# Four graph layers on one core: two of three batch norms folded early, the last batch's bias and norm by halves

## The chip, the cores and the metric

The kernel runs on one NeuronCore of a Trainium2 chip. The metric is the device time of one execution in microseconds. The core has five engines with their own in-order queues: PE (TensorE: matmuls and transposes, writing to PSUM), DVE (VectorE), ACT (ScalarE), POOL (GpSimd) and SP (which here only issues DMAs). In the profile, PEld is PE's weight load, listed apart.

## The reference, cut to what matters

Sixteen graphs ("batches") of 1024 nodes with 128 features go through four layers; each layer's result is added to its input and normalised over the features.

```python
x = layernorm(x + L0(x, adj))           # attention over neighbours, gated
x = layernorm(x + L1(x, adj, nodemask)) # dilated adjacency, three SAGE steps with batch norm
x = layernorm(x + L2(x, adj))           # attention over neighbours, gated
x = layernorm(x + L3(x, adj))           # two-step graph convolution with elu
```

The change concerns layer 1's output and the very end of layer 3:

```python
h1 = bn(relu(sage(x,  adj_d, ...)), g1, be1)   # bn: mean and variance over all batches and nodes
h2 = bn(relu(sage(h1, adj_d, ...)), g2, be2)
h3 = bn(relu(sage(h2, adj_d, ...)), g3, be3)
y  = concat([h1, h2, h3], -1) @ Wl + bl        # then layernorm(x + y)
...
out = norm_A @ (h @ W2) + b2                   # layer 3, then layernorm(x + out)
```

A batch norm is, once its statistics are known, a scale and a shift of each feature: h = a * n + s. So the product with Wl is n @ (a * Wl) plus a constant s @ Wl, which belongs to the bias.

## The kernel before

Each batch is held as 8 blocks of 128 rows, either by rows ("xn", "yn", "n": 128 partitions x 8 x 128) or transposed ("hT", "yT", "xT": 128 x 1024). Most work on a batch goes by two halves of 512 columns, one PSUM bank each. The helpers `turned` (L753: transposes through PE), `products` (L761: matmuls with a 128x128 weight) and `halves` (L747) yield one such half after another; `spans(fine)` (L803) yields two halves or the whole. `normed` (L786) is the layer norm: statistics and aggregates on DVE, the power -1/2 on POOL, then one ACT activation for each block of 128 rows.

Each layer is written as a few streams for each batch (Python generators) which `take_turns` and `in_turn` (L810, L814) interleave. The order written there is not yet the order on an engine: a scheduler in the tile framework arranges the instructions of each engine, and waits for buffers follow from pools of a fixed number of tiles.

Layer 1's third step (`Step`, loop over the 16 batches in the order 8 to 15, 0 to 7) has for each batch: load hT and ag on SP's queue (L1348, L1350); `out` (L1388 and after) with 32 matmuls of 128x128 (L1397), bias on DVE ("o", L1399), squares on ACT (L1405), row sums ("ss", L1406), "rn" (L743, power on POOL at L744, L1409) and "n" (L1413); `keep` (L1417 and after) with transposes (L758), copies "nT" (L1422), batch norm statistics (L1423) and a store of nT to DRAM (h2T_d, L1424, on POOL's queue). After all batches `norm` (L1325) turns the statistics into bn_ab[2], whose column 0 is the scale and column 1 the shift (L1327 to L1332). bn_ab[0] and bn_ab[1] have been known since the first and second step.

`Layers23` holds what layers 2 and 3 need. Its weights are loaded during layer 1's third step (`weights`, L1200), and `load` (L1229) brings a batch: adjacency A8, the three un-normed outputs hb0, hb1, hb2 (one buffer each, so a batch's hb can be loaded only when the products of the batch before have read it), and xn. `take_norms` (L1220) folds the three norms into bias and Wl: three matmuls into "pc" (L1224), an addition to blcol (L1225), three scalings of Wl (L1227).

Layer 2's `before` for a batch is: products of Wl with hb (L1547), yT with the bias (L1548), transposes, yn and xn (L1551, L1554), layer norm, then xT, hT, G and hn for the attention. Two batches run `before` at the start of layer 2, with attention behind. `attention` uses the PSUM pool ps_w for "pmm" and ps_a for "acc"; everything else goes through ps_h (tag "h", two banks). In layer 1, ps_h has four banks and ps_a four.

At the end of layer 3 (`after`), `propagated` gives "prop" by halves (L1536, L1538), one ACT instruction adds the bias c2 (L1667), then prop is transposed and added to xn (L1670), normed, and stored (L1673; for the last batch by halves, on SP's queue).

Of the kernel before, what the change touches and what calls it, by code (L numbers as in the profile page):

```python
# [9 lines left out]
F32 = mybir.dt.float32  # L10
# [6 lines left out]
AF = mybir.ActivationFunctionType  # L17
OP = mybir.AluOpType
AX = mybir.AxisListType
PSUM = bass.MemoryType.PSUM  # L20
DRAM = bass.MemoryType.DRAM

P = 128
# [616 lines left out]
def fast_kernel(ctx: ExitStack, tc: tile.TileContext, t: dict, out: bass.AP, flag: bass.AP):  # L640

    nc = tc.nc
    B, N, D = t["x"].shape
    NT = N // P
    H2 = N // 512
# [40 lines left out]
    def nat(ap):  # L686
        return ap.rearrange("(t p) d -> p t d", p=P)
# [7 lines left out]
    def column(pool, src, name):  # L695
        v = pool.tile([P, 1], F32, name=name)
        nc.sync.dma_start(v, bass.AP(tensor=src.tensor, offset=src.offset, ap=[[1, P], [1, 1]]))
        return v
# [62 lines left out]
    def products(psum, *pairs):  # L761

        for p, c, _ in halves(psum):
            for i, (W, x) in enumerate(pairs):
                nc.tensor.matmul(p, W, x[:, c], start=(i == 0), stop=(i == len(pairs) - 1))  # L765
            yield p, c
# [16 lines left out]

        return v[:, :, None].to_broadcast([P, 4, P])

    def normed(small, r, fine=False):  # L786

        for k in spans(fine):
            n = k.stop - k.start
            st = small.tile([P, NT, 6], F32, name="ln_st")  # L790
            mv = small.tile([P, NT, 2], F32, name="ln_mv")
            for i in range(n):
                nc.vector.bn_stats(st[:, i, :], r[:, k.start + i, :])  # L793
            for i in range(n):
                nc.vector.bn_aggr(mv[:, i, :], st[:, i, :])
            rstd = power_mhalf(small, mv[:, :n, 1], add=LN_EPS, name="ln_rstd")
            nb = small.tile([P, NT], F32, name="ln_nb")
            nc.vector.scalar_tensor_tensor(nb[:, :n], mv[:, :n, 0], -1.0, rstd, op0=OP.mult, op1=OP.mult)  # L798
            for i in range(n):
                nc.scalar.activation(r[:, k.start + i, :], r[:, k.start + i, :], AF.Identity,  # L800
                                     scale=rstd[:, i:i + 1], bias=nb[:, i:i + 1])

    def spans(fine):  # L803

        return [slice(0, NT // 2), slice(NT // 2, NT)] if fine else [slice(0, NT)]
# [384 lines left out]
    class Layers23:  # L1190
# [8 lines left out]
        def weights(self, ps_h):  # L1199
            wts = self.wts  # L1200
            self.Wl = wts.tile([P, 3, P], F32, name="Wl")
            nc.sync.dma_start(self.Wl, nat(t["L1_gnn_Wl"]))
            self.blcol = column(wts, t["L1_gnn_bl"], "blcol")
            self.W2T = transposed(wts, ps_h, matrix(wts, t["L2_gnn_W_w"], "l2W"), "l2WT", "h")
            self.b2 = column(wts, t["L2_gnn_W_b"], "l2b")
            self.As2 = symmetric(wts, ps_h, matrix(wts, t["L2_gnn_A"], "l2A"), "l2As", "h")
            self.gw = wts.tile([P, 2, 32], F32, name="l2gw")
            nc.vector.memset(self.gw, 0.0)
            self.gb = wts.tile([P, 3], F32, name="l2gb")
            for i, n in enumerate(("ig", "fg", "og")):  # L1210
                with nc.allow_non_contiguous_dma(reason="a vector of 256"):
                    nc.sync.dma_start(self.gw[:, :, i], t[f"L2_gnn_{n}_w"].rearrange("o (h d) -> d (o h)", d=P))
                src = t[f"L2_gnn_{n}_b"]
                nc.sync.dma_start(self.gb[:, i:i + 1], bass.AP(tensor=src.tensor, offset=src.offset, ap=[[0, P], [1, 1]]))
            self.U = [matrix(wts, t[f"L3_gnn_W{i}"], f"U{i}") for i in range(3)]
            self.c = [column(wts, t[f"L3_gnn_b{i}"], f"c{i}") for i in range(3)]
            self.nbig = wts.tile([P, 1], F32, name="nbig")
            nc.vector.memset(self.nbig, -BIG)

        def take_norms(self, psum):  # L1220

            pc = psum.tile([P, 1], F32, name="pc", tag="h")
            for l in range(3):
                nc.tensor.matmul(pc, self.Wl[:, l, :], bn_ab[l][:, 1:2], start=(l == 0), stop=(l == 2))  # L1224
            nc.vector.tensor_add(self.blcol, self.blcol, pc)  # L1225
            for l in range(3):
                nc.vector.tensor_scalar(self.Wl[:, l, :], self.Wl[:, l, :], bn_ab[l][:, 0:1], None, op0=OP.mult)  # L1227

        def load(self, s, b):  # L1229
            s.A8 = self.ins.tile([P, NT, N], FP8, name="A8", bufs=3)  # L1230
# [255 lines left out]
    with ExitStack() as ph:  # L1486
        work = ph.enter_context(tc.tile_pool(name="l2_work", bufs=1, reuse_waits="tile"))
        small = ph.enter_context(tc.tile_pool(name="l2_small", bufs=3, reuse_waits="tile"))
        ps_w = ph.enter_context(tc.tile_pool(name="l2_pw", bufs=2, space=PSUM, reuse_waits="tile"))
        ps_a = ph.enter_context(tc.tile_pool(name="l2_pa", bufs=1, space=PSUM, reuse_waits="tile"))  # L1490
        ps_h = ph.enter_context(tc.tile_pool(name="l2_ph", bufs=2, space=PSUM, reuse_waits="tile"))

        W2T, b2, As2, gw, gb, nbig, blcol, Wl = l2.W2T, l2.b2, l2.As2, l2.gw, l2.gb, l2.nbig, l2.blcol, l2.Wl
        (U0, U1, U2), (c0, c1, c2) = l2.U, l2.c
# [46 lines left out]
        def before(s, b):  # L1541

            if b:
                l2.load(s, b)
            yield
            yT = wide("yT")
            for p, c in products(ps_h, *((Wl[:, l, :], s.hb[l]) for l in range(3))):  # L1547
                nc.scalar.activation(yT[:, c], p, AF.Identity, bias=blcol)  # L1548
            yn = rows("yn", 2)
            for p, c, k in turned(ps_h, yT):  # L1550
                nc.vector.tensor_mul(yn[:, k, :], tiles3(p), half_rows(mf[:, b * NT + k.start:b * NT + k.stop]))  # L1551

            for k in spans(b < 2):
                nc.vector.tensor_add(s.xn[:, k, :], s.xn[:, k, :], yn[:, k, :])  # L1554
            yield
            normed(small, s.xn, b < 2)
            yield
            s.xT = wide("xT", 2)
            for p, c, _ in turned(ps_h, s.xn):
                nc.scalar.copy(s.xT[:, c], p)  # L1560
            yield
            s.hT = wide("hT", 2)
            for p, c in products(ps_h, (W2T, s.xT)):
                nc.scalar.activation(s.hT[:, c], p, AF.Identity, bias=b2)
            yield
            s.G = wide("G", 2)
            for p, c in products(ps_h, (As2, s.hT)):
                nc.scalar.copy(s.G[:, c], p)
            s.hn = wide("hn", 2)
            for p, c, _ in turned(ps_h, s.hT):  # L1570
                nc.vector.tensor_copy(s.hn[:, c], p)
            yield
# [31 lines left out]
        def after(s, b):  # L1604
# [14 lines left out]
            last = b == B - 1  # L1619
# [44 lines left out]
            parts = scaled_parts(h2, U2, db)  # L1664
            yield
            r = propagated(parts, A, dB)
            nc.scalar.activation(r, r, AF.Identity, bias=c2)  # L1667
            yield
            for p, c, k in turned(ps_h, r):
                nc.vector.tensor_add(s.xn[:, k, :], s.xn[:, k, :], tiles3(p))  # L1670
            normed(small, s.xn, last)
            for k in spans(last):
                (nc.sync if last else nc.gpsimd).dma_start(nat(out[b])[:, k, :], s.xn[:, k, :])  # L1673
            yield
# [49 lines left out]
```

## Time and profile before

| | |
|---|---|
| median of 4 runs | 3015.39 us (3008.26 to 3020.5) |
| profiled execution | 3010.69 us |
| its span, first to last instruction | 3009.0 us |
| mean granted TensorE clock | 0.972 |
| busy: PE, DVE, ACT, POOL | 91%, 77%, 67%, 11% |
| chain that ended last: PE, DVE, issue, ACT, DMA, POOL | 37%, 22%, 21%, 9%, 6%, 5% |

All durations are from the one profiled execution; its time is the span and 1.7 us around it. A busy share is a mean over stages that have different limits, so what a place costs is read in that place: in the timeline (start, duration, engine, line, output<-inputs, and in brackets how long the engine had been idle and for whom it waited) and in the chain of waits, which goes back from the last instruction to whatever released each step. A PE row with "x2" for one product of 128x512 is one matmul: the f32 product is recorded as two.

### The profile page before, as it was taken

To read this page: it belongs to the slowest core of one execution; us is meant where nothing else is said; L and a number is where in the kernel's file an instruction comes from. 1 tells how busy PE (TensorE), PEld (TensorE's weight loads), DVE (VectorE), ACT (ScalarE), POOL (GpSimd) and SP (SyncE) were. 2 spreads that over 40 slices of the span, in tenths; PEclk is the share of its full clock that TensorE was granted. 3 is DMA by queue.
4 is the path that set the end of the run, shared out by engine and by line. 5 is a ranking of instruction groups with operands and counts; after the bars stand their busy time and mean duration, and the time that the engine had idled before them with its cause. 6 is when DMAs were issued, how large, how long until landed. Compare 5 with 4: busy or idle time off the path is not lost.

```text
span 3009.0 us, 42998 instructions
## 1 busy us (share of the span) xinstructions
PE 2737.2 (91%) x15219; PEld 1719.9 (57%) x15282; DVE 2329.7 (77%) x5987; ACT 2028.2 (67%) x3475; POOL 326.0 (11%) x295
## 2 busy tenths in 40 slices
PE   7999999996999998998999987999999999999995
PEld 3444444443566666887788874455555555555554
DVE  6898898887999995776688885766777777777765
ACT  5777787784788777666555535766666676676763
POOL 0000000003000001121122231000010001000000
PEclk9999999998999999999999998999999999999998
DMA  5344444431000014223367692111111111111000
GB/s 163 126 161 148 133 147 154 147 128 42 2 2 2 2 76 164 90 99 128 128 238 243 229 350 88 36 56 57 63 70 60 64 69 68 56 57 57 22 15 23
DMA packets 124128, 297.96 MB, mean 99 GB/s; under 512 B 12672, under 2 KB 65664, under 8 KB 116736
## 3 DMA queue, kind: packets, MB, share of 16 engines
q1 hardware_dynamic: 103440, 211.65, 21.1%
q0 software_dynamic: 20464, 83.47, 7.4%
q8 instruction: 122, 2.00, 0.3%
q14 instruction: 102, 0.84, 0.1%
HBM read 211.04 MB, written 84.02 MB: 98 GB/s over the span
## 4 chain that ended last, share of the span: by engine, by line
PE 37%; DVE 22%; issue 21%; ACT 9%; DMA 6%; POOL 5%; SPq 0%; POOLq 0%; DVEq 0%; ACTq 0%
PE ph L1536 8%; PE acc L1293 7%; PE ph L765 5%; PE acc L1601 4%; DMA an<-in_adj 4%; PE ph L1397 3%; PE pmm L723 3%; POOL ln_rstd L744 3%; ACT xn L800 3%; DVE ln_st L793 3%; PE ph L758 3%; PE ph L1522 2%; DVE em L1587 2%; ACT em L969 2%; PE acc L976 2%
## 5 line engine op out<-in xcount | busy, mean ns | idle before, releaser
L723 PE MATMUL pmm<-G,hT 128*128 128x512 f32 x1024 | 506.0, 611 | 7.7 <-DVE mx L1587 5.0
L800 ACT ACTIVATE xn<-xn,ln_nb,ln_rstd 128x128 f32<-128x128 f32 x512 | 207.6, 481 | 115.5 <-DVE ln_nb L798 115.5
L723 PEld LDWEIGHTS pmm<-G,hT 128*128 128x128 f32 x1024 | 179.1, 193 | 175.9 <-issue 140.5
L976 PE MATMUL acc<-em,hs 128*128 128x512 f32 x512 | 244.8, 602 | 16.4 <-DVE hs L973 14.3
L1293 PE MATMUL acc<-a,lo 128*128 128x512 f32 x768 | 243.4, 401 | 16.0 <-DVE lo L1260 16.0
L744 POOL TENSOR_TENSOR ln_rstd<-ln_rstd,mhalf 128x8 f32<-128x8 f32 (+1 forms) x68 | 113.5, 1670 | 1327.5 <-DVE ln_rstd L741 607.6
L1601 PE MATMUL acc<-em,hs 128*128 128x512 f32 x512 | 250.4, 608 | 3.6 <-DVE hs L1598 1.9
L1293 PE MATMUL acc<-a,hi 128*128 128x512 f32 x768 | 244.0, 402 | 3.7 <-ACT hi L1259 3.5
L1140 ACT ACTIVATE q<-s,negc 128x512 f16<-128x512 f32 x256 | 170.4, 696 | 59.6 <-DVE negc L1119 22.3
L922 ACT ACTIVATE ab<-an 128x1024 bf16<-128x1024 f32 x128 | 134.6, 1052 | 109.6 <-DMA an<-in_adj 71.0
L1138 PE MATMUL s<-step,carry 128*128 128x384 bf16 (+3 forms) x1034 | 199.4, 304 | 7.9 <-DVE carry L1108 3.2
L1152 ACT ACTIVATE carry<-pc,negone 128x512 fp8e4<-128x512 f32 x256 | 166.6, 698 | 38.5 <-PE pc L1151 29.1
L965 DVE CUSTOM_DVE_ANT_0 em<-pmm,msk 128x1024 f32<-128x1024 f32 x128 | 156.1, 1219 | 31.5 <-PE acc L976 26.3
L1293 PEld LDWEIGHTS acc<-a,lo 128*128 128x128 f32 x768 | 144.1, 190 | 55.2 <-DVE lo L1260 21.6
L1587 DVE CUSTOM_DVE_ANT_0 em<-pmm,msk 128x1024 f32<-128x1024 f32 x128 | 155.8, 1217 | 25.7 <-PE acc L1601 21.2
L925 DVE SCALAR_TENSOR_TENSOR chk<-an 128x1024 fp8e4<-128x1024 f32 x128 | 156.4, 1222 | 17.4 <-DMA an<-in_adj 17.1
L1293 PEld LDWEIGHTS acc<-a,hi 128*128 128x128 f32 x768 | 143.0, 190 | 37.1 <-ACT hi L1259 4.0
L1582 ACT ACTIVATE msk<-A,nbig 128x1024 bf16<-128x1024 fp8e4 x128 | 145.8, 1140 | 26.7 <-DVE mx L1587 23.4
L930 DVE TENSOR_SCALAR carry<-pt 128x1024 fp8e4<-128x1024 bf16 x128 | 155.7, 1217 | 6.8 <-PE pt L929 6.8
L1397 PE MATMUL ph<-Wx,hT 128*128 128x128 f32 x768 | 152.1, 281 | 5.0 <-DVE l2WT L709 3.2
L976 PEld LDWEIGHTS acc<-em,hs 128*128 128x128 f32 x512 | 91.2, 191 | 113.2 <-issue 87.8
L969 ACT ACTIVATE em<-em,nmx 128x1024 f32<-128x1024 f32 x128 | 146.8, 1147 | 12.3 <-DVE nmx L967 11.8
(289 smaller groups left out, 6256.6 us busy)
## 6 DMA issues: line engine op xcount, KB each, us to landing
an<-in_adj SPq DMA_DIRECT2D x128, 512.0 KB, 4.2
adj_d<-carry POOLq DMA_DIRECT2D x16, 1024.0 KB, 5.0
A<-dil_d SPq DMA_DIRECT2D x16, 1024.0 KB, 6.7
rdeg<-rdeg_d SPq DMA_DIRECT2D x32, 512.0 KB, 4.3
ag_d<-ag POOLq DMA_DIRECT2D x32, 512.0 KB, 5.3
ag<-ag_d SPq DMA_DIRECT2D x32, 512.0 KB, 6.0
A<-adj_d SPq DMA_DIRECT2D x16, 1024.0 KB, 4.7
xn<-in_x SPq DMA_DIRECT2D x16, 512.0 KB, 4.2
```

Source lines behind the costliest of these rows:

```text
L723: nc.tensor.matmul(p[:, h * 512:(h + 1) * 512], lhsT, rhs[:, h * 512:(h + 1) * 512], start=True, stop=True)
L744: nc.gpsimd.tensor_tensor(r, r, mhalf[:, :n], op=OP.pow)
L800: nc.scalar.activation(r[:, k.start + i, :], r[:, k.start + i, :], AF.Identity, scale=rstd[:, i:i + 1], bias=nb[:, i:i + 1])
L969: nc.scalar.activation(em, em, AF.Exp, bias=nmx, accum_out=sm)
L976: nc.tensor.matmul(s.acc[:, c], hs, em[:, c], start=(jt == 0), stop=(jt == NT - 1))
L1138: nc.tensor.matmul(s[:, lo or 0:], y, twos if lo is None else step[:, :512 - lo], start=(j == 0), stop=(j == len(terms) - 1))
L1140: nc.scalar.activation(q[:, h * 512:(h + 1) * 512], s, AF.Abs, bias=st.negc[:, i:i + 1])
L1293: nc.tensor.matmul(acc, part[:, jt, :], pieces[h * NT // 2 + i][:, j, :], start=(jt == 0 and p == 0), stop=(jt == NT - 1 and p == 1))
L1397: nc.tensor.matmul(p[:, i * P:(i + 1) * P], x[:, j * P:(j + 1) * P], W, start=(n == 0), stop=(n == 1))
L1536: nc.tensor.matmul(p, part[:, jt, :], A[:, jt, c], start=(jt == 0 and i == 0), stop=(jt == NT - 1 and i == 1))
L1587: nc.vector.tensor_tensor_reduce(em, e, msk, 1.0, 0.0, op0=OP.add, op1=OP.max, accum_out=mx)
L1601: nc.tensor.matmul(s.acc[:, c], hs, em[:, c], start=(jt == 0), stop=(jt == NT - 1))
```

## The change

It has four parts.

1. `weights` keeps a copy of Wl in a new tile "shift" and scales the parts of Wl for the first two norms at once (`scaled`), in layer 1's third step. `take_norms` does this for the third norm and takes the copy for the products into pc.
2. For the first two batches, `before` takes one two-bank tile "py" from ps_w in place of two tiles from ps_h, and multiplies hb0 and hb1 into both halves ahead of hb2.
3. In layer 2 the pool ps_w is opened after ps_a and ps_h, so that it lies in banks 4 to 7, those of layer 1's ps_a, and no longer in 0 to 3.
4. For the last batch, the bias c2 is added by halves, and each half is normed directly after its addition to xn.

```diff
-    def normed(small, r, fine=False):
+    def normed(small, r, fine=False, pieces=None):
-        for k in spans(fine):
+        for k in pieces or spans(fine):
...
             nc.sync.dma_start(self.Wl, nat(t["L1_gnn_Wl"]))
+            self.shift = wts.tile([P, 3, P], F32, name="shift")
...
             self.c = [column(wts, t[f"L3_gnn_b{i}"], f"c{i}") for i in range(3)]
+            for l in range(2):
+                self.scaled(l)
...
+        def scaled(self, l):
+            nc.vector.tensor_copy(self.shift[:, l, :], self.Wl[:, l, :])
+            nc.vector.tensor_scalar(self.Wl[:, l, :], self.Wl[:, l, :], bn_ab[l][:, 0:1], None, op0=OP.mult)
+
         def take_norms(self, psum):
             pc = psum.tile([P, 1], F32, name="pc", tag="h")
+            self.scaled(2)
             for l in range(3):
-                nc.tensor.matmul(pc, self.Wl[:, l, :], bn_ab[l][:, 1:2], start=(l == 0), stop=(l == 2))
+                nc.tensor.matmul(pc, self.shift[:, l, :], bn_ab[l][:, 1:2], start=(l == 0), stop=(l == 2))
             nc.vector.tensor_add(self.blcol, self.blcol, pc)
-            for l in range(3):
-                nc.vector.tensor_scalar(self.Wl[:, l, :], self.Wl[:, l, :], bn_ab[l][:, 0:1], None, op0=OP.mult)
...
-        ps_w = ph.enter_context(tc.tile_pool(name="l2_pw", bufs=2, space=PSUM, reuse_waits="tile"))
         ps_a = ph.enter_context(tc.tile_pool(name="l2_pa", bufs=1, space=PSUM, reuse_waits="tile"))
         ps_h = ph.enter_context(tc.tile_pool(name="l2_ph", bufs=2, space=PSUM, reuse_waits="tile"))
+        ps_w = ph.enter_context(tc.tile_pool(name="l2_pw", bufs=2, space=PSUM, reuse_waits="tile"))
...
-            for p, c in products(ps_h, *((Wl[:, l, :], s.hb[l]) for l in range(3))):
+            if b < 2:
+                p = ps_w.tile([P, N], F32, name="py", tag="w")
+                cs = [slice(h * 512, (h + 1) * 512) for h in range(H2)]
+                for ls in ((0, 1), (2,)):
+                    for c in cs:
+                        for l in ls:
+                            nc.tensor.matmul(p[:, c], Wl[:, l, :], s.hb[l][:, c], start=(l == 0), stop=(l == 2))
+                turns = [(p[:, c], c) for c in cs]
+            else:
+                turns = products(ps_h, *((Wl[:, l, :], s.hb[l]) for l in range(3)))
+            for p, c in turns:
                 nc.scalar.activation(yT[:, c], p, AF.Identity, bias=blcol)
...
             r = propagated(parts, A, dB)
-            nc.scalar.activation(r, r, AF.Identity, bias=c2)
+            for k in spans(last):
+                c = slice(k.start * P, k.stop * P)
+                nc.scalar.activation(r[:, c], r[:, c], AF.Identity, bias=c2)
             yield
             for p, c, k in turned(ps_h, r):
                 nc.vector.tensor_add(s.xn[:, k, :], s.xn[:, k, :], tiles3(p))
-            normed(small, s.xn, last)
+                if last:
+                    normed(small, s.xn, pieces=[k])
+            if not last:
+                normed(small, s.xn)
```

In the order that the scheduler gives the changed program, the products of hb0 and hb1 for both batches, eight in all, stand on PE between the transposes of layer 1's last batches. Before, only the first half's two for the first batch stood there. The loads of hb0 and hb1 of the second batch stand on SP's queue directly behind layer 1's last load.

## The prediction

> **What bounds the kernel now.** I read the page's busy shares first, then the table of stretches around the end of layer 1, then the chain of waits there, and last the timeline of the final 20 us. The edits touch three places only: the last 60 us of layer 1, the join of layers 1 and 2 (about 1828 to 1856 us), and the end. All other rows keep their order on every engine.
>
> ```profile
> PE 2737.2 (91%) x15219; PEld 1719.9 (57%) x15282; DVE 2329.7 (77%) x5987; ACT 2028.2 (67%) x3475; POOL 326.0 (11%) x295
> ```
>
> TensorE is busy 91% of the span, but not at the edited places. In the stretches below (us, busy us and instructions of PE, PEld, DVE, ACT, POOL, then clock, DMA share, GB/s) it falls to 3.45 of 10 us before the join, and the granted clock to 0.74. In 1770 to 1790 the DMA engines are full.
>
> ```profile
> 1770.00:1790.00 20.00, 17.68 (x132) 14.86 (x132) 17.42 (x34) 7.09 (x14) 6.54 (x6) 1.00 1.03 377
> ...
> 1820.00:1830.00 10.00, 3.45 (x16) 2.80 (x16) 6.88 (x14) 3.48 (x6) 4.30 (x5) 0.74 0.32 128
> 1830.00:1845.00 15.00, 12.67 (x30) 5.68 (x30) 6.29 (x32) 5.52 (x11) 2.02 (x2) 0.83 0.56 195
> ```
>
> The chain of waits in order of time (start us, us, what) shows what the join costs: statistics, norm, pc, eight records on PE, two layer norms, the second batch's yT, its norm, and only then layer 2's first products.
>
> ```profile
> 1776.32 7.95 DMA hb<-h1T_d
> ...
> 1827.33 0.70 DVE stats L1423
> 1828.05 1.03 DVE bmv L1327
> 1829.35 0.58 POOL brstd L744
> 1830.56 0.60 PE pc L1224 x2
> 1831.39 5.52 PE ph L765 x8
> ...
> 1843.43 1.02 POOL ln_rstd L744
> 1844.69 0.38 issue
> 1845.07 0.68 ACT yT L1548
> ...
> 1853.71 0.50 ACT xn L800
> 1854.25 1.63 PE ph L758 x4
> 1855.88 7.31 PE ph L765 x12
> ```
>
> At the end (timeline) the whole-width bias waits for both halves of prop, and PE sits idle 2.03 us:
>
> ```profile
> 2991.74 0.69 DVE L1538 TENSOR_TENSOR prop<-ph,dB 128x512 f32<-128x512 f32 x1 [2.25 <-PE ph L1536]
> 2992.52 1.15 ACT L1667 ACTIVATE prop<-prop,c 128x1024 f32<-128x1024 f32 x1 [6.90 <-DVE prop L1538]
> ...
> 2993.72 1.09 PE L758 MATMUL ph<-identf,prop 128*128 128x128 f32 x8 [2.03 <-ACT prop L1667]
> ...
> 3000.63 1.65 ACT L800 ACTIVATE xn<-xn,ln_nb,ln_rstd 128x128 f32<-128x128 f32 x4 [0.56 <-DVE ln_nb L798]
> ```
>
> **The change part by part**, in the profiled execution's time (3010.69 us, span 3009.0; the median of the four runs, 3015.39, lies 4.70 above it). Below, (0) and (1) are the batches.
>
> *Copies and early scaling.* Three 128x128 copies into shift are new. The nearest row is the 128x128 copy of L709, 0.28 us, followed 0.20 us later by the next instruction. With two Wl scalings moved forward they stand on DVE behind the memsets of 1732.1. Wl was issued at 1725.9 and landed in 4.0 us, so nothing waits for it, and DVE idles 0.73 and 1.76 us nearby. Cost 0; without that cover 3 x 0.20 = 0.6 us.
>
> *The swapped PSUM pools* give py the banks of layer 1's accumulators, free since its second step. Cost 0. On the banks of ph the early products would queue behind layer 1's transposes; nothing in the trace prices that.
>
> *Early products.* A 128x512 f32 product is two records, 0.43 us apart at full clock and 0.86 in the throttled rows: 0.86 or 1.72 us. Before, two stand early (1780.45, 1784.32); after, eight do, each behind a group of transposes, in both batches. Of the six new ones, the first two fall before 1799.67, where PE waits for DVE's l2WT anyway; the last two fall into the 4.79 us of PE idle before 1822.08. The third and fourth stand at 1806.6 and 1811.6 where PE has only 0.24 us free, so each pushes the next group by 0.86 - 0.24 = 0.6 us. hb0(1) must be there at 1806.6: SP can issue it at 1795.4, the place of the xn load before, and xn loads landed in 8.3 to 10.6 us, so 1803.7 to 1806.0: just in time. The share of DMA is down to 0.22 after 1810.
>
> *Order in the tail.* On DVE the last batch's rn now stands behind the statistics of the batch before it, and on POOL behind that batch's store of h2T. Walking the new order with the old durations (n 0.60 a half, o 0.60, ss 0.60, statistics 0.60, POOL 1.66 plus 0.25 to reach it, transposes 0.66, nT 0.59): the rn of the sixth batch of eight goes 0.7 earlier, at 1808.85; the seventh at 1815.85, POOL until 1817.8, n until 1819.25; its statistics end at 1823.45; the last rn at 1823.5, POOL until 1825.45, n until 1826.9, statistics until 1828.95. Before, the aggregate began at 1828.05: **+0.9**. Bounds: -1.0 if the last n no longer waits behind statistics, as it did from 1823.5 to 1825.28, and +2.9 if POOL's three waits (1.9 each) are all bare where before 2.8 us were.
>
> *SP's queue.* The xn(0) load, issued at 1777.5, now stands behind the next hT and ag (1780.42, 1781.16). PE stands still 1.29 us at 1784.32 for the hb load that shares the full DMA with it; at 377 GB/s its 0.52 MB is 1.4 us. Between 0 and -1.3 I take **-0.7**.
>
> *The join.* Counted from a bn_ab scale at the same time: Wl's third scaling (0.28) ends at 1830.62, where before pc and the bias came first. PE: 1.72 for half 0, until 1832.45; pc 0.3; blcol 1833.1; 1.72 for half 1, until 1834.5; transposes of both halves until 1836.1 (before 1838.35); layer norm of (0) about 2 us earlier. hb2(1) can be issued at 1834.6 (before 1836.94), behind hb0(2), hb1(2) and dB on SP, which wait for nothing later; it takes the median of the hb loads, 4.0 us: 1838.7. Its two products end at 1842.2, yT(1) at 1843.1, its transposes 1843.85, yn and xn 1845.7, statistics and POOL twice as before: the last xn(1) starts at 1850.55 instead of 1853.71. ACT now does yT(1) ahead of all eight xn(0); these end at 1846.4, earlier than before, so nothing is late. **-3.1**.
>
> The clock decides here. Row: after PE's 3.22 us of idle to 1799.67 its records stood 0.42 us apart where 0.22 is usual, so a short gap already throttled it. The Trainium skill's page "TensorE: Matmul & The Clock Gate", section "What's actually happening", speaks of half clock only after an idle window of about 3.4 us, and the gap ahead of hb2(1)'s products is 1838.7 - 1836.1 = 2.6: by the rule they run at full clock, 1.7 us less, and the join gives -4.8. The page's section "Why this matters for your kernels" wants no gaps of over some 3 us between bursts; cutting one run of products into bursts, as here, goes against that. I take the row (throttled, -3.1), since windows run freely and the bursts are short.
>
> *The end.* Bias of half 0 (ACT idle) is done before PE finishes half 1 at 2991.5. So: transposes of half 0 until 2992.2; DVE prop until 2992.4, add 2993.1, four statistics 2993.9, aggregates 2994.2, add of half 1 2994.85, rstd, POOL 2995.1 to 2996.1 (before 2997.17). Half 1's four statistics all stand behind nb now: 2997.1, aggregates, rstd, POOL 2997.85 to 2998.85, last xn at 2999.1 to 2999.2 against 3000.63: **-1.45**. The store's 6.7 us behind it stay. Two halves of bias instead of one cost 0.69 x 2 against 1.15, hidden. If DVE's new order stalls at the second add, 0.6 of it goes.
>
> Sum: 0.9 - 0.7 - 3.1 - 1.45 = -4.35, so 3006.3 in the profiled execution and **3011.0** on the median.
>
> **The rivals.** *All pieces fall well.* Products of the join at full clock, hb2(1) in 3.4 us (the fastest hb load), so batch (1) is bound by DVE: nb(0) at 1840.7, its yn to 1842.1, last xn(1) at 1848.05, -5.7; tail -1.0; SP -1.3; end -1.45; together -9.45, 3005.9. If the first layer 2 products also find the clock up (x8 took 5.41 us against 8 x 0.43 = 3.44), -11.4, 3004. For it: PE has work in the gaps of the tail. Against it: clock 0.74 and 0.77 around the join.
>
> *The tail costs more than the join gives: slower.* In-order DVE is the mechanism: rn of the last batch cannot pass the statistics of the seventh, which wait for PE's transposes behind a product. Price: +2.9 for bare POOL waits, +1.7 for a throttled product in front of the transposes, +2 if hb0(1) misses 1806.6 (PE in order, every later batch behind it). From +4.6 on, join and end are eaten; with all three +6.6, and if hb2(1) takes the 8.0 us that hb1(0) took, +4 more: +10.6 - 5.25 = +5.4, 3021. For it: DVE is in the chain all through the tail. Against it: DMA is nearly idle after 1810.
>
> *The early products do not happen early*: then only the end is left, -1.45, 3014. In the program's order they do stand early, so this is part of the forecast's range.
>
> **How the numbers follow.** Chances: forecast 0.43 (its own range 3007 to 3014.5), all well 0.37, slower 0.20. A difference of 0.3% (9 us) is about what a measurement of this kernel can tell from no change. Nearly all of the second case and a fifth of the first, with the spread of the runs (3008 to 3020), lie beyond it: 0.44 faster. Of the third, 0.17 slower. The rest, 0.39, within. The range takes the good case to 3001 and the bad one to 3020.
>
> **What would show it.** Right: eight py records between 1780 and 1823; hb loads of (1) before 1800; hb2(1) issued within 4.5 us of the bn_ab scale; yT(0) some 2 us and the last xn(1) some 3 us nearer to the aggregate; the end's PE idle of 2.03 us gone and the distance from the last prop to the last xn (8.9 us before) down to 7.4. Wrong: PE waiting on DMA for hb at a py record; the aggregate more than 2 us later; yT(1) holding up xn(0).

## The result, and the profile after

The changed kernel takes 3010.46 us (median of 42 runs, 3002.77 to 3020.82) where the kernel before takes 3014.38 (63 runs beside it, 3002.73 to 3025.84): ratio 0.9988, 95% interval 0.9982 to 0.9994. It is 4 us faster, 0.12%. The forecast was 3011.0. The sum came out; the experiments show that two of its terms were wrong by 5 to 7 us each, with opposite signs.

The profiled execution takes 3007.53 us, its span is 3005.8 (before 3010.69 and 3009.0). Of the 3.2 us, 1.80 are not the change's: the aggregate of the second norm, ahead of all edited instructions, already starts at 1717.25 instead of 1719.05. In the profiles below that instruction lies anywhere from 1710.6 to 1721.2. So stretches inside each profile are compared: the third step (aggregate of the second norm to aggregate of the third), its tail (from the first "n" of its tenth batch, on DVE, to the same aggregate), the join (from there to the first product with l2WT), and the end (last prop to last xn).

The stretches of the changed kernel (us; busy us and instructions of PE, PEld, DVE, ACT, POOL; clock; DMA share; GB/s):

```profile
1770.00:1790.00 20.00, 17.18 (x129) 14.54 (x128) 16.17 (x32) 7.03 (x14) 5.63 (x7) 1.00 1.02 396
...
1820.00:1830.00 10.00, 2.62 (x12) 2.53 (x12) 6.21 (x12) 2.48 (x5) 3.22 (x4) 0.65 0.58 231
1830.00:1845.00 15.00, 11.81 (x26) 5.90 (x26) 6.78 (x33) 6.12 (x12) 2.16 (x3) 0.50 0.29 97
```

Read the clock column in the last row: 0.50 in these 15 us of the join, where before it was 0.83. PE is busy nearly as long as before in that row (11.81 and 12.67 us), with fewer instructions: they are slower. The chain of waits of the changed kernel, in order of time:

```profile
1774.17 9.20 DMA hb<-h1T_d
1783.41 1.13 PE py L1563 x2
...
1828.27 1.03 DVE bmv L1335
...
1830.52 0.21 DVE Wl L1227
1830.77 2.07 PE py L1563 x2
1832.84 0.22 PE pc L1234 x2
1833.06 1.93 PE py L1563 x2
1835.01 3.47 DMA hb<-h2T_d
1838.52 3.79 PE py L1563 x4
1842.40 0.69 ACT yT L1568
1843.14 1.98 PE ph L758 x8
...
1851.77 0.50 ACT xn L800
...
1853.94 7.32 PE ph L765 x12
```

The second batch's hb2 is now a link of the chain: the load can start only when the first batch's last product has read the buffer. From the aggregate to the last xn of batch (1) it is 23.50 us (before 25.66), to l2WT 25.67 (before 27.82). At the end (timeline), half 0 is biased while PE still multiplies half 1 and transposed directly behind it, and the last xn comes 7.16 us behind the last prop (before 8.89):

```profile
2987.62 0.72 ACT L1689 ACTIVATE prop<-prop,c 128x512 f32<-128x512 f32 x1 [3.92 <-DVE prop L1547]
2989.59 0.60 PE L758 MATMUL ph<-identf,prop 128*128 128x128 f32 x4
2989.78 0.69 DVE L1547 TENSOR_TENSOR prop<-ph,dB 128x512 f32<-128x512 f32 x1 [2.26 <-PE ph L1545]
...
2991.28 0.65 PE L758 MATMUL ph<-identf,prop 128*128 128x128 f32 x4 [1.10 <-ACT prop L1689]
...
2996.94 1.65 ACT L800 ACTIVATE xn<-xn,ln_nb,ln_rstd 128x128 f32<-128x128 f32 x4 [0.98 <-DVE ln_nb L798]
```

### The profile page after: what moved, and what is told of

Read it like the earlier page. It is cut to its first block, busy times and chain, and to the rows that moved or that the text cites. A ratio compares the mean times of both kernels' runs of the same rounds, so it can differ in the third digit from the quotient of the medians.

```text
span 3005.8 us, 43001 instructions
## 1 busy us (share of the span) xinstructions
PE 2739.2 (91%) x15219; PEld 1720.3 (57%) x15282; DVE 2330.0 (78%) x5990; ACT 2026.8 (67%) x3476; POOL 325.6 (11%) x295
## 4 chain that ended last, share of the span: by engine, by line
PE 37%; DVE 23%; issue 21%; ACT 9%; POOL 5%; DMA 5%; POOLq 0%; SPq 0%; ACTq 0%; DVEq 0%
PE ph L1545 8%; PE acc L1301 6%; PE ph L765 5%; PE acc L1621 4%; PE pmm L723 4%; POOL ln_rstd L744 3%; DMA an<-in_adj 3%; DVE ln_st L793 3%; ACT xn L800 3%; PE ph L758 3%; PE ph L1405 2%; PE ph L1531 2%; DVE em L1607 2%; PE acc L976 2%; ACT em L969 2%
## 5 line engine op out<-in xcount | busy, mean ns | idle before, releaser
L744 POOL TENSOR_TENSOR ln_rstd<-ln_rstd,mhalf 128x8 f32<-128x8 f32 (+1 forms) x68 | 113.5, 1670 | 1322.0 <-DVE nmx L1609 607.0
L925 DVE SCALAR_TENSOR_TENSOR chk<-an 128x1024 fp8e4<-128x1024 f32 x128 | 156.4, 1222 | 17.5 <-DMA an<-in_adj 16.7
```

The source lines that it names most:

```text
L744: nc.gpsimd.tensor_tensor(r, r, mhalf[:, :n], op=OP.pow)
```

## The experiments

All stretches in one table (us, from each kernel's one profile; "early" is the number of 128x512 products that PE has between layer 1's own matmuls of the third step; ratios are to the kernel before, measured beside it, with 95% intervals).

| kernel | early | third step | its tail | join | end | ratio |
|---|---|---|---|---|---|---|
| before | 2 | 109.00 | 42.57 | 27.82 | 8.89 | 1 |
| changed | 8 | 111.02 | 44.95 | 25.67 | 7.16 | 0.9988 (0.9982 to 0.9994) |
| e1, part 4 alone | 2 | 113.52 | 45.55 | 29.32 | 7.15 | 0.9996 (0.9987 to 1.0005) |
| e2, without part 4 | 8 | 111.82 | 44.37 | 25.66 | 8.90 | 0.9997 (0.9988 to 1.0007) |
| e3, early for (0) only | 4 | 112.24 | 44.62 | 25.45 | 7.15 | 0.9984 (0.9976 to 0.9993) |
| e4, one-bank tiles | 8 | 112.07 | 44.47 | 24.28 | 7.16 | 0.9989 (0.9980 to 0.9998) |
| e5, added matmuls | 7 | 114.07 | 46.31 | 25.82 | 7.16 | 0.9987 (0.9977 to 0.9996) |
| e6, parts 1 and 3 | 0 | 106.34 | 38.83 | 26.86 | 8.90 | 0.9980 (0.9971 to 0.9990) |
| e8, (0) only, one-bank tiles | 4 | 109.97 | 42.65 | 24.50 | 7.15 | 0.9976 (0.9966 to 0.9985) |
| e9, one-bank tiles, added matmuls | 7 | 112.35 | 46.29 | 23.74 | 7.16 | 0.9973 (0.9962 to 0.9985) |
| e10, without part 2 | 0 | 104.93 | 38.88 | 26.78 | 7.16 | 0.9968 (0.9956 to 0.9980) |
| e12, part 3 alone | 0 | 106.68 | 39.02 | 27.91 | 8.90 | 0.9978 (0.9968 to 0.9987) |
| e11, (0) by norm, in ps_h | 0 | 105.04 | 38.98 | 26.67 | 7.16 | 0.9971 (0.9960 to 0.9981) |
| e13, the same, added matmuls | 0 | 108.00 | 40.43 | 25.93 | 7.16 | 0.9958 (0.9942 to 0.9974) |

In e5 and e9 the eighth product stands behind the last transposes, and nine added matmuls lie inside the tail, as in e13.

**Each half of the change by itself.** e1 takes the edits of `normed`, the bias and the last norm alone (part 4); e2 takes all the others.

> The kernel before with part 4 of the change alone (bias and norm of the last batch by halves). Theory of the prediction: last prop to last xn goes from 8.89 us to about 7.2 to 7.4, everything ahead of it stays as in the kernel before (hb1's product to aggregate 43.7, aggregate to last xn of batch (1) 25.7), the time falls by 1.5 us: ratio 0.9995, which its interval can only just tell from 1. Rival: the stores behind the last norm take longer when the halves come closer together (the stretch from last xn to the end of the span grew by 0.5 us in the changed kernel), and what is left is 1 us or less.

> The changed kernel without part 4. Theory: hb1's product to aggregate 44.8 us as in the changed kernel (before 43.7), aggregate to last xn of batch (1) 23.5 (before 25.7), last prop to last xn 8.9; the sum of the first two is 1 us better than before, ratio 0.9995 or so. hb1's load of batch (0) shows whether its 9.2 us (before 8.0) repeats: with the order of the loads as the cause it is over 8.8 us again, with chance in the transfers it falls to about 8. Rival: the tail gives back all that the join brings, ratio 1.0000 or above.

The end does what was worked out, and a little more: 7.15 or 7.16 us in all ten profiles that have part 4, 8.89 or 8.90 in the four that have not. The stretch behind the last xn, where e1's rival looked, is 8.2 to 9.2 us long with part 4 and 8.1 to 8.9 without, so little of it comes back there. In the times e1 is 0.04% faster, inside its interval. e2 is not told apart from the kernel before. hb1's load settles a small point: in e1, which has the order of loads of the kernel before, issue to product took 9.4 us (1774.06 to 1783.49), in the kernel before 8.0, in the changed kernel 9.2, in e2 8.7. The order of the loads is no cause that can be seen; 8.0 was the odd one. e1's third step, 4.5 us longer than that of the kernel before with the same order on every engine, warns against reading this stretch from one pair of profiles; 3.0 us of the 4.5 lie in the tail.

**The second batch, and the tile of two banks.** e3 changes one digit; e4 gives every half a tile of its own, from a pool that is closed before the attention's is opened in its banks.

```diff
-            if b < 2:
+            if b < 1:
```

> The changed kernel with early products for batch (0) alone; batch (1) has all three products in one place as before. Theory of the prediction (four more products on PE and the order that they bring on DVE and POOL lengthen the tail): hb1's product to aggregate falls back from 44.9 to about 43.7 to 44.0; the join grows, since four products of batch (1) move back behind the aggregate (4 x 1.0 us at full clock, 4 x 2.06 at half): aggregate to last xn of batch (1) 26 to 30 us instead of 23.5; sum: 2 to 5 us slower than the changed kernel. Rival: the tail's length has nothing to do with batch (1)'s early products; it stays at 44.9. Second rival: with PE busier behind the aggregate the clock comes up as it did before (0.99 from 5 us after its start), and the join is not longer than 25.7.

```diff
+        ps_e = early_ctx.enter_context(tc.tile_pool(name="l2_pe", bufs=4, space=PSUM, reuse_waits="tile"))
...
-                p = ps_w.tile([P, N], F32, name="py", tag="w")
...
+                turns = [(p, c) for p, c, _ in halves(ps_e, "e")]
...
```

> The changed kernel with the early products in four tiles of one bank in place of two tiles of two banks; the banks go to the attention's pool once both batches are through. Theory A (yT's first half waits for both halves because the tile is one): yT of batch (0) starts 2 us sooner after the aggregate (4.9 us in place of 6.75), its transposes follow the products with no idle in place of 0.78; last xn of batch (0) about 1 us sooner. Theory B (the join's end hangs on hb2's load of batch (1), issued when the products of batch (0) have read the buffer and 3.5 us on its way): last xn of batch (1) stays at 23.5 us after the aggregate to within 0.3, ratio to the changed kernel 1.000; by A alone it would be 22.5.

In e3 the four products of batch (1) that went back behind the aggregate cost the join nothing (25.45 us, changed kernel 25.67), so the second rival stands: PE's run of products is longer, and from 1840.25 on they are 0.43 us apart. The stretch ahead of it did not get shorter either: hb1's product to the aggregate is 44.9 us (44.86 in the changed kernel). That the order on DVE and POOL, which in e3 is nearly that of the kernel before, lengthens the tail falls with it.

e4 shows the wait for the whole tile. In the changed kernel both halves of yT start together, 6.75 us behind the aggregate, when the second product ends; with tiles of one bank the first starts at 5.04. Timeline of the changed kernel:

```profile
1830.77 2.07 PE L1563 MATMUL py<-hb,Wl 128*128 128x512 f32 x2 [3.24 <-DVE Wl L1227]
...
1832.92 2.06 PE L1563 MATMUL py<-hb,Wl 128*128 128x512 f32 x2
...
1835.02 1.26 ACT L1568 ACTIVATE yT<-py,blcol 128x512 f32<-128x512 f32 x2 [6.37 <-PE py L1563]
```

and of e4 (aggregate at 1831.57):

```profile
1834.08 2.08 PE L1564 MATMUL ph<-hb,Wl 128*128 128x512 f32 x2 [3.24 <-DVE Wl L1227]
...
1836.24 2.05 PE L1564 MATMUL ph<-hb,Wl 128*128 128x512 f32 x2
1836.61 0.69 ACT L1568 ACTIVATE yT<-ph,blcol 128x512 f32<-128x512 f32 x1 [5.79 <-DVE blcol L1235]
...
1841.73 1.98 PE L1564 MATMUL ph<-hb,Wl 128*128 128x512 f32 x4 [1.54 <-DMA hb<-h2T_d]
```

The join is 1.4 us shorter, though hb2(1) comes no sooner (10.16 us behind the aggregate, changed kernel 10.25): the products waiting for it take 1.98 us in place of 3.78, because the clock is up. The last xn of batch (1) starts 22.1 us behind the aggregate, so theory B, by which the load would have held it at 23.5, is out. In the time the 1.4 us do not show.

**Is it the clock?** e5 adds 15 matmuls whose result is not used, 9 in front of the last batch's transposes, 6 in front of the products with hb2:

```diff
+        def warm(self, psum, n):
+            pw = psum.tile([P, 512], F32, name="pw", tag="h")
+            for i in range(n):
+                nc.tensor.matmul(pw[:, :256], identf, self.shift[:, 0:2, :].rearrange("p a d -> p (a d)"), start=True, stop=True)
...
+            self.warm(psum, 6)
...
+                if self.l == 2 and b == order[-1]:
+                    l2.warm(ps_h, 9)
```

> The changed kernel with 15 added matmuls of 128x256 (f32, on the copy of Wl; their result is not used): 9 in PE's idle ahead of the last batch's transposes, 6 behind them ahead of the products with hb2. Theory A (the join's matmuls run at half clock because PE is idle for 5.3 us ahead of the last transposes and 3.2 us behind them): with the gaps filled the granted clock between 1820 and 1845 us is 0.9 or more in place of 0.50 to 0.65; a product of 128x512 takes 1.02 to 1.08 us in place of 2.06, eight transposes 1.05 in place of 1.97; aggregate to the first matmul of layer 2's next weights (l2WT) falls from 25.7 to about 22.5, and the stretch from the last out matmul to the aggregate from 12.9 to about 12. Time 3 to 4 us less than the changed kernel, ratio to before 0.9975. Theory B (the clock does not follow PE's idle in these few us): the clock stays near 0.5; the added matmuls take 1.03 us each, the last six end 3 us after the scaling of Wl, and the join is 2 to 3 us longer than in the changed kernel.

> Four one-bank tiles and the 15 added matmuls together. If both theories hold, clock by idle and wait for the whole tile: yT's first half 4 us behind the aggregate, last xn of batch (1) 20 us behind it, l2WT at 22 us (changed kernel 25.7), limited by hb2's load of batch (1), issued a matmul of 1 us sooner and 3.5 us on its way; ratio to before 0.9970 to 0.9978, faster than the changed kernel by 3 to 5 us. If the clock stays low, as with the added matmuls alone: 2 us slower than the one-bank tiles without them.

Stretches of e5 (columns as above):

```profile
1822.50:1825.00 2.50, 2.02 (x11) 1.63 (x11) 2.50 (x5) 1.60 (x3) 0.28 (x1) 1.00 0.77 228
...
1830.00:1835.00 5.00, 4.91 (x25) 3.84 (x25) 3.19 (x10) 3.36 (x6) 1.16 (x2) 1.00 0.47 111
...
1840.00:1845.00 5.00, 3.52 (x4) 0.96 (x4) 2.68 (x16) 0.28 (x1) 1.02 (x1) 0.66 0.01 6
```

and PE's timeline of e5 (aggregate at 1831.87):

```profile
1834.70 1.96 PE L1571 MATMUL py<-hb,Wl 128*128 128x512 f32 x4
1837.44 1.23 PE L758 MATMUL ph<-identf,yT 128*128 128x128 f32 x8 [0.78 <-ACT yT L1576]
1841.10 3.52 PE L1571 MATMUL py<-hb,Wl 128*128 128x512 f32 x4 [2.43 <-DMA hb<-h2T_d]
```

Theory A holds as to the clock: 1.00 with the gaps filled, four records in 1.96 us where the changed kernel needs 2.07 for two, yT at 4.83 us behind the aggregate in place of 6.75. It fails as to the time: hb2(1) takes 4.4 us on its way now, PE idles 2.43 us for it, the clock is lost again, and l2WT comes at 25.82, no sooner than in the changed kernel. With one-bank tiles added (e9) it is 23.74; there PE still waits 2.60 us for hb2(1). In both, the third step is no shorter. So half clock and the tile's wait cost the join some 2 us together.

**Which part brings the time?** e6 has parts 1 and 3 only: the loop condition of part 2 is never met, and part 4 is left out.

> The kernel before with parts 1 and 3 alone: Wl copied and scaled early, the pool of the attention opened last; the products are in one place as before, and so are the end's bias and norm. Theory of the prediction: both are covered, and the loads of hT and ag ahead of xn of batch (0) follow from these parts too: ratio 1.000, last out matmul to aggregate 12.4 to 12.9, aggregate to l2WT 27.8 to 29.3 as in the two profiles with the order of before. For hb1's load of batch (0), whose issue to product took 8.0 us before and 9.4 in the kernel with the end alone, which has the same order of loads: 8.7 to 9.5 says that 8.0 was the odd one and that the order of the loads brings nothing. Rival: the early parts alone bring what the join brought, ratio 0.9993.

The rival, and well beyond it: 0.9980, more than the whole change brings, with the shortest third step until then. What part 3 does is seen in the order on PE. It opens ps_w last, so layer 2's ps_h lies in the banks of layer 1's ps_h, which are in use until the last transposes are copied. In the kernel before, ps_h lay in banks that layer 1 no longer used, and two products of batch (0) had slipped into the middle of the third step (1780.45 and 1784.32). With part 3 none does: in e6 PE has no product with hb ahead of the last transposes. e8 has four early products left, in one-bank tiles (its diff, cut, is against e4):

```diff
-        ps_e = early_ctx.enter_context(tc.tile_pool(name="l2_pe", bufs=4, space=PSUM, reuse_waits="tile"))
+        ps_e = early_ctx.enter_context(tc.tile_pool(name="l2_pe", bufs=2, space=PSUM, reuse_waits="tile"))
...
-            if b < 2:
+            if b < 1:
...
```

> The changed kernel with early products for batch (0) alone, in two tiles of one bank; batch (1) has its products in one place as before. With both halves of batch (0) apart, yT's first half starts at about 5.0 us behind the aggregate (as with four one-bank tiles) and not at 6.75. Theory A (the wait for the whole tile and the clock are what costs; the place of batch (1)'s products does not matter, since its hb2 arrives 10 us after the aggregate in any case): aggregate to l2WT 24.3 to 24.6 in place of 25.5 to 25.7; ratio to before 0.9984. Rival: six products of batch (1) behind the transposes cost more when the clock comes up late: l2WT at 26 us or more.

It confirms the tile's wait (first yT at 5.02, join 24.50) and that batch (1) gains nothing from being early. Then the new theory, that early products cost time, was put to the test: part 2 taken out of the changed kernel (e10, its condition is never met), and part 3 put alone into the kernel before (e12), which is one line moved:

```diff
-        ps_w = ph.enter_context(tc.tile_pool(name="l2_pw", bufs=2, space=PSUM, reuse_waits="tile"))
         ps_a = ph.enter_context(tc.tile_pool(name="l2_pa", bufs=1, space=PSUM, reuse_waits="tile"))
         ps_h = ph.enter_context(tc.tile_pool(name="l2_ph", bufs=2, space=PSUM, reuse_waits="tile"))
+        ps_w = ph.enter_context(tc.tile_pool(name="l2_pw", bufs=2, space=PSUM, reuse_waits="tile"))
```

> The changed kernel without part 2: no tile py, every batch has its products in one place through ps_h. Since ps_h's banks are those of layer 1's ps_h until the last transposes are read (part 3), no product can run during the third step; the first products of batch (0) come behind the last transposes. Theory (new, from the run with parts 1 and 3 alone): a product in the middle of the third step is not free: PE is that step's bound, 1.02 us for each product, and the wait for hb1's load of 1.3 to 2.9 us stands in PE's queue ahead of the step's own matmuls. So aggregate of the second norm to aggregate of the third is about 106.3 us in place of 111 to 112, aggregate to l2WT about 27 in place of 25.7, the end 7.15: 3 to 4 us less than the changed kernel, ratio to before 0.9975. Rival (the prediction's: the early products lie in PE's idle time): the third step's 106.3 was chance, this kernel is 1 to 2 us slower than the changed one, ratio 0.9993.

> The kernel before with part 3 alone: the attention's PSUM pool is opened last, nothing else is changed. The kernel before ran two products of batch (0) in the middle of the third step (from banks that layer 1 no longer used); with part 3 they move behind it. Theory (products in the middle of the step cost): third step 106 to 107 us in place of 109 to 113.5, one or two products more behind the aggregate, with the scaling of Wl ahead of them: aggregate to l2WT 28 to 30; ratio 0.9985. Rival A (the prediction: moving the pool is worth nothing): ratio 1.000. Rival B (the gain of parts 1 and 3 together was the early scaling, which lets products run while the third norm is worked out): third step 106, but the join 4 us longer, ratio 1.000.

Both come out on the theory's side, and e10 and e12 by more than it said (0.9968 and 0.9978 for 0.9975 and 0.9985). Part 3 alone is 0.22% faster than the kernel before, some 6.6 us, and the changed kernel without part 2 is 0.32% faster. Part 2 by itself therefore costs: changed against e10, 0.9988/0.9968 = 1.0020; e2 against e6, 0.9997/0.9980 = 1.0017, each with some 0.0013 of uncertainty: 5 to 6 us. The third step says the same: 104.9 to 106.7 us in the four kernels with no early product and nothing added, 109.0 to 113.5 in the seven with two, four or eight. That part 3 also gives all of layer 2 other banks is no rival: from the join's end to the last prop it is 1135.86 us before, 1136.96 in e12 and 1136.27 in e10.

The tail shows it more clearly. Ahead of it the step takes 66.0 to 66.4 us or 67.3 to 68.0, and kernels with and without early products have both. In the kernel before and in e12 the tail runs from the first line to the second:

```profile
1785.48 1.28 DVE L1413 SCALAR_TENSOR_TENSOR n<-o,rn 128x512 f32<-128x512 f32 x2
...
1828.05 1.02 DVE L1327 BATCH_NORM_AGGREGATE bmv<-stats 128x2 f32<-128x192 f32 x1
```

```profile
1787.14 1.28 DVE L1413 SCALAR_TENSOR_TENSOR n<-o,rn 128x512 f32<-128x512 f32 x2
...
1826.16 1.01 DVE L1327 BATCH_NORM_AGGREGATE bmv<-stats 128x2 f32<-128x192 f32 x1
```

It takes 38.8 to 39.0 us in all four kernels with no early product and nothing added. With two it is 3.6 and 6.6 us longer, with four 3.7 and 5.7, with eight 5.4 to 6.0. So early products cost time, but not in step with their number. (Four products fewer hardly show in the times either: e3 against the changed kernel 0.9996, e8 against e4 0.9987, each with 0.0010 to 0.0013 of uncertainty.)

For eight products, why is read in PE's waits. In 1775 to 1826 us, the changed kernel (engine, line, what it waited for: us in all, times, longest):

```profile
PE ph L758 <- DVE n L1421: 5.9, 3, 5.3
PE py L1563 <- DMA hb<-h1T_d: 2.6, 1, 2.6
PE wtr L708 <- ACT nT L1430: 1.4, 1, 1.4
PE ph L1405 <- DVE l2WT L709: 1.3, 1, 1.3
```

the kernel before:

```profile
PE ph L758 <- DVE n L1413: 5.3, 3, 4.8
PE ph L1397 <- DVE l2WT L709: 3.2, 1, 3.2
PE ph L765 <- DMA hb<-h1T_d: 1.3, 1, 1.3
```

and e12, part 3 alone:

```profile
PE ph L758 <- DVE n L1413: 7.9, 5, 3.5
PE ph L1397 <- ACT nT L1422: 1.3, 1, 1.3
PE ph L1397 <- DVE l2WT L709: 1.2, 1, 1.2
```

e12 has no wait for hb at all. Over the whole third step PE's idle times add up to 16.7 us with eight early products (changed kernel) and 16.3 and 16.9 without any (e12, e10): the products filled no idle time. What the wait for n loses (10.0 us in e10 to 7.8) the wait for hb1's load takes (2.56). PE's busy time in the step goes from 87.5 and 89.1 us (e10, e12) to 93.2 to 94.6 (changed kernel, e2, e4), and the step grows by as much. Eight products 0.86 us long are 6.9 us; the 1 us or so that is missing is not accounted for. For two products this working falls short. They are 1.7 us of PE time, and the wait for hb1's load is 1.3 us in the kernel before and 2.7 in e1. Some 2 us more lie between the eleventh batch's n and the last one's, where these kernels have no early product (29.4 and 28.8 us; 27.0 to 27.1 in the four kernels without). There DVE and POOL have another order with part 3, and PE waits 3.2 us for l2WT before and 1.2 in e12. How much of part 3's 6.6 us is the products and how much is this order, no run separates.

Two more looked for a version that uses the idle time near the aggregate.

```diff
-            if b < 2:
+            if b < 1:
...
+                turns = [(p, c) for p, c, _ in halves(ps_h)]
+                for ls in ((0, 1), (2,)):
+                    for p, c in turns:
+                        for l in ls:
+                            nc.tensor.matmul(p, Wl[:, l, :], s.hb[l][:, c], start=(l == 0), stop=(l == 2))
```

> As the kernel without part 2, but for batch (0) the products of hb0 and hb1 with both halves stand ahead of those of hb2, in two banks of ps_h. They run in the 3.2 us in which PE waited for the third norm. Theory: three to four products of 1.0 to 2.06 us fill that gap; yT's second half comes 1 to 2 us sooner after the aggregate than without (7.8), l2WT at 26 us or less; ratio 0.9972. Rival (half clock: four products take 8 us, more than the gap): first half of yT later than 4.9, l2WT unchanged at 27.

> The same with nine added matmuls of 128x256 (result not used) in PE's idle ahead of the last transposes, which kept the granted clock at 1.00 in the run with added matmuls on the changed kernel. Theory: last out matmul to aggregate 12.25 or less, products at 1.02 us from the first on, yT's halves at 4 and 5 us after the aggregate, l2WT at 24 to 25 us unless the loads of hb for batch (1) come last; ratio 0.9965 to 0.9970. Rival (the added matmuls only move the stall to hb's loads of batch (1), 4 us and more on their way each): l2WT 26 to 27, no faster than without them.

e11's order of instructions turned out to be that of e10 on every engine: the scheduler ran the products of e10 in that gap already. So it says nothing on its theory and is a second measurement of e10, 3005.33 us after 3004.96. The timeline of e10 (aggregate at 1826.09) shows the gap filled; compare the changed kernel, in which PE idles 3.24 us there:

```profile
1825.39 1.01 PE L1234 MATMUL pc<-bn_ab,shift 128*128 128x1 f32 x4 [0.68 <-ACT nT L1430]
...
1826.26 4.31 PE L765 MATMUL ph<-hb,Wl 128*128 128x512 f32 x6
...
1830.91 0.69 ACT L1568 ACTIVATE yT<-ph,blcol 128x512 f32<-128x512 f32 x1 [5.58 <-DVE blcol L1235]
1830.93 2.84 PE L765 MATMUL ph<-hb,Wl 128*128 128x512 f32 x6 [0.25 <-DVE blcol L1235]
```

The products of batch (0) run while the aggregate and the norm are worked out, yT starts 4.82 us behind the aggregate, and the clock is up from 1829.55 on. e13, which has e11's edit and nine added matmuls, has the lowest time of all (3000.55 us, of 5 runs), but its interval takes in e10's ratio, and its profile gives no reason: the join is 0.9 us shorter (25.93, between its theory's 24 to 25 and its rival's 26 to 27), the third step 3 us longer. Its profile is 9.2 us shorter than e10's, but it is 10.6 us ahead already at the aggregate of the second norm, where the two kernels are the same. It is not told apart from e10. Either of e10 and e13 beats both kernels.

## Why the prediction was right

- *Sum and end result*: 3011.0 against 3010.46. Right in size, but not for its reasons.
- *The swapped PSUM pools, "Cost 0"*: this step failed. It was priced by what the new banks allow to py, not by what they take from ph. Part 3 alone brings 6.6 us (e12; its interval is 3.9 to 9.6): two products leave the middle of the third step, and DVE and POOL get another order there. "On the banks of ph the early products would queue behind layer 1's transposes; nothing in the trace prices that" named the better place and set it aside.
- *Early products and the order in the tail, +0.9, and SP's queue, -0.7*: failed as a price of part 2. The 0.6 us by which each of two products was to push the next group is no term of the sum. Against the kernel with part 3 they cost 5 to 6 us. Three covers were named and did not hold: the wait for l2WT (3.2 us before) is 1.3 in the changed kernel; the idle ahead of the last transposes stayed, 5.34 us behind two more products, since it belongs to the chain over DVE and POOL; and hb1's load, which the moved xn load was to speed up, still keeps PE waiting 2.56 us. Since the kernel before held two such products itself, pool and early products nearly cancel, and the forecast of the two together, +0.2, looks right. The walk along DVE and POOL gave +0.9 and hb1's product to the aggregate grew by 1.13, but e3 has nearly the old order there and the same 44.9 us, and e1 has 45.25 with the order of before: the agreement was chance.
- *The join, -3.1*: right in kind, somewhat too large; -2.15 by l2WT, -2.16 by the last xn. The missing 1 us is the half 0 that did not go ahead of half 1: py is waited for as one tile (e4: 1.4 us). hb2(1) was foreseen 10.65 us behind the aggregate and came at 10.25. The choice of the row (throttled) over the page's rule was right, though not for the gap that it named: the gap ahead of hb2(1)'s products was 0.80 us in place of 2.6, and the clock had been at 0.50 since the 5.34 us of idle ahead of the last transposes and stayed there until 1846.82.
- *The end, -1.45*: right, -1.73.
- *Copies and early scaling, 0*: right. The next ss stands where it stood, and e6, which has them, is no slower than e12 (0.9980 and 0.9978).
- *The rivals*: "slower" named the tail as its place. The tail does cost, by 5 to 6 us where it asked for 4.6 and more, but part 3 had paid for it.
- *The signs*: most came: eight py records from 1778.29 to 1818.55, the loads of hb0(1) and hb1(1) at 1794.08 and 1795.45, the shorter end. yT(0) is only 0.4 us nearer to the aggregate, not 2 (6.75 and 7.16 us), and the last xn(1) 2.16, not 3. One sign of being wrong came too: PE waits for hb at a py record, 2.56 us where before it was 1.29.

## What to carry to other kernels

Work pulled forward is free only if it lands in idle time that it can fill. Here PE stood still for 16 to 17 us of the stage, but 8 to 10 of these were waits for n, at the end of a chain over DVE and POOL, and what the early products took from them the wait for a load gave back, so the products came on top. When a tile moves to other banks, ask also which instructions may now run earlier or no longer can. When a sum comes out right, undo its terms one by one before believing them. And look for a stretch that repeats from profile to profile: here the tail showed what the scatter of the whole third step hid.

## What the runs showed of the hardware

The granted clock changes on a grid of 3.41 us. In the changed kernel it falls at 1822.93 us, rises at 1846.82, falls at 1850.24 and rises at 1857.06, which is 7, 1 and 2 times 3.41 us apart; in the kernel before it falls at 1828.26, rises at 1835.09 and falls at 1852.16, 2 and 5 times. Stretches of this grid, in the changed kernel and then in e5 (columns as above):

```profile
1829.76:1833.17 3.41, 2.40 (x5) 1.36 (x6) 0.65 (x5) 0.00 (x0) 0.37 (x1) 0.50 0.40 163
1833.17:1836.58 3.41, 2.63 (x6) 1.06 (x7) 0.15 (x2) 1.56 (x3) 0.00 (x0) 0.50 0.15 24
...
1843.41:1846.82 3.41, 3.39 (x16) 2.52 (x15) 2.53 (x5) 3.41 (x10) 0.68 (x1) 0.50 0.44 144
1846.82:1850.24 3.42, 0.33 (x3) 0.14 (x2) 2.59 (x20) 1.49 (x4) 1.01 (x1) 1.00 0.01 2
```

```profile
1837.99:1841.40 3.41, 0.98 (x6) 0.72 (x6) 3.27 (x9) 1.10 (x2) 0.00 (x0) 1.00 0.38 137
1841.40:1844.82 3.42, 3.22 (x4) 0.67 (x2) 1.28 (x11) 0.10 (x1) 1.02 (x1) 0.50 0.00 0
```

So the place of a gap counts, not its length alone. PE's run of 4.2 us without a gap (1830.77 to 1834.98) lies across two stretches, fills neither and does not release the clock; the first stretch that PE fills (3.39 us busy) is followed by full clock. In the kernel before that stretch was 1831.68 to 1835.09, busy throughout, and so the join had full clock from there to 1852.16. In e5 2.43 us of idle fell into one stretch and half clock followed; in the changed kernel the 2.56 us ahead of 1783.41 fell across two (2.09 and 1.98 us busy), and the clock stayed at 1.00. The Trainium skill's page "TensorE: Matmul & The Clock Gate", section "What's actually happening", speaks of an idle window of about 3.4 us; the grid agrees, but the window need not be idle throughout, since 0.98 us of it were busy in e5. No limit comes out: a stretch with 2.60 us busy was followed by half clock (e12, from 2555.69), one with 1.42 by full clock (e10, from 2068.20).

Two profiles of the same order of instructions differ by 4.5 us in the third step (before, e1), where the DMA engines are busy 80% of the time in the kernel before and full from 1770 to 1790. A difference of that size in the whole step, between two single profiles, shows nothing.
